# Cross-attention block on one core: W2 from seven block products a step later, exponentials by head, mask added in PSUM

## The chip, the cores and the metric

The kernel runs on one core of a Trainium2 chip. The metric is device microseconds of one execution. Its engines have in-order queues of their own: PE (matmuls and weight loads), DVE, ACT, POOL (elementwise work; POOL does not touch PSUM here), and SP, which issues most DMAs. PSUM is used as eight banks of 128 partitions by 512 float32 values, called b0 to b7 below. All data are float32.

## The reference, cut to what matters

128 sequences of 128 tokens and 256 channels, 16 heads of 16 channels, hidden width 1024:

```python
q, k, v = heads(x @ Wq + bq), heads(ctx @ Wk + bk), heads(ctx @ Wv + bv)
scores = where(j < i, q @ k.T / 4, -1e30)      # strictly below the diagonal
attn = softmax(scores); attn[row 0] = 0
x1 = layer_norm(x + (attn @ v) @ Wo + bo, ln1_g, ln1_b)
out = layer_norm(x1 + relu(x1 @ W1 + b1) @ W2 + b2, ln2_g, ln2_b)
```

## The kernel before, in words

Two sequences make a pair `p`, so there are 64 pairs. The order of every engine's instructions is the order of the calls in the text, written by hand; each engine takes its own in that order and waits for what it needs. The kernel is a pipeline over pairs: `step(p)` (L995), for p from 5 to 63, does the scores and softmax of pair p, the attention output of p-2, the hidden layer and the product with W2 of p-3, the second normalization of p-4 and the store of p-5. `third`, `fourth` and `fifth` fill the pipeline, and the lines from L1056 on empty it.

PE's order in a step is: `weigh(p-2)` (attention times values, L471 and L481, into bank 7), `scores_both(p)` (L364), `queries(p+1)` (bank 4), `attention_out(p-2)` (bank 5), `keys(p+1)` (bank 0), `values(p)` (bank 1), `hidden(p-3)` (L687, banks 2, 3, 4, 0), `second(p-3)` (L705, bank 6). The scores are split: the "high" half are the later 64 queries against all 128 keys (banks 0 to 3, four heads in each), the "low" half the first 64 queries against 64 keys (banks 6, 7, 4, 5). Rows of both sequences share the 128 partitions.

The softmax goes through all engines. `mask` (L378, DVE) adds 0 or -1e30 and copies the scores from PSUM to the tile `sm`; `maximum` is a row maximum on DVE (L389) and then a subtraction on POOL (L390); `exponential` (L397, ACT) takes 1024 elements a row at once, so three instructions serve 16 heads of both halves; `sums` adds the rows and inverts the sums on DVE (L409, L410) and multiplies on POOL (L411). `turn` (L424, DVE) transposes blocks of 32, and `bring` (L439, SP) moves them between partitions by 16 DMAs into `pT`, which `weigh` reads two steps later.

ACT also empties banks: queries (L268), keys (L279, four, each with a tile as bias and one as scale), values (L299, L304), the hidden layer's relu (L693); and it applies the normalizations `norm1` (L542) and `norm2` (L579). `turn_x1` (L651, DVE) transposes what `norm1` made, and SP's DMAs take it over DRAM to `x1T`, which `hidden` reads a step later. `second` multiplies the hidden tile `hT` (one buffer; 8 chunks of 128 channels by 256 tokens) with W2: for each of the two sequences 8 matmuls of 256 columns, summed in bank 6. `second_sum` (L715, DVE) adds the residual `x1b`, `stats` makes the mean and variance, `scale_and_shift` (POOL) the factors, `finish` (POOL) the gain and offset of the second normalization, `store` the output's DMA. In steps 28 and 51 `pad` puts empty instructions between the matmuls of `second`.

Of the kernel before, what the change touches and what calls it, by code (L numbers as in the profile page):

```python
# [8 lines left out]
F32 = mybir.dt.float32  # L9
# [4 lines left out]
P = 128  # L14
# [5 lines left out]
def tile_cross_attention_block(  # L20
# [192 lines left out]
    def bank(name):  # L213
        turns[0] += 1
        return at_bank(4 + turns[0] % 4, name)
# [179 lines left out]
    def exponential(p, hi, part):  # L395
        sm = states[p]["sm", hi]
        nc.scalar.activation(sm[:, part, :], sm[:, part, :], AF.Exp)  # L397
# [20 lines left out]
    def turn(p, hi, t):  # L418

        st = states[p]  # L420
        if "tb" not in st:
            st["tb"] = wide(f"tb_{p}").rearrange("p (j n) -> p j n", j=NS)
        at = (t if hi else 2) * 256
        nc.vector.transpose(  # L424
            st["tb"][:, :, at : at + 256].rearrange("p j (n a) -> p n j a", a=32),
            st["sm", hi].rearrange("p h j -> p (h j)")[:, t * 1024 : (t + 1) * 1024].rearrange(
                "p (n j a) -> p n j a", j=NS, a=32
            ),
        )
# [139 lines left out]
    def scale_and_shift(p):  # L569

        st = states[p]
        deviation(p, 2)
        shift(p, 2)
# [126 lines left out]
    def second(p, s, fs=range(FC), pad=0):  # L700
        st = states[p]
        if s == 0 and fs[0] == 0:
            st["py"] = at_bank(6, f"py_{p}")
        for f in fs:
            nc.tensor.matmul(  # L705
                st["py"][:, s * D : (s + 1) * D], st["hT"][:, f, s * P : (s + 1) * P],
                w2[:, f, :], start=(f == 0), stop=(f == FC - 1),
            )
            for _ in range(pad):
                nc.tensor.nop(hint="pad", nofuse=True)  # L710

    def second_sum(p):
        st = states[p]
        t2 = st["t2"] = ffn.tile([P, 2, D], F32, tag="t2", name=f"t2_{p}")
        nc.vector.tensor_tensor(  # L715
            t2, st.pop("py").rearrange("p (s d) -> p s d", s=2), st.pop("x1b"), ALU.add
        )
# [3 lines left out]

    warm = bank("warm")
    for i in range(12):
        nc.tensor.transpose(warm[:, i % 4 * P : (i % 4 + 1) * P], ident, ident)
# [237 lines left out]
    def fifth():  # L964
        p = 4
        load_ahead(p)
        scores_both(p)
        mask(p, 0, B)
        mask(p, 1, A)
        maximum(p, 1, ONE)  # L970
        queries(p + 1)
        mask(p, 1, B)
        maximum(p, 1, TWO)
        exponential(p, 1, ONE)
        mask(p, 0, A)
# [12 lines left out]
        second(1, 1)  # L988
        turn(p, 1, 0)
        turn(p, 1, 1)  # L990
        turn(p, 0, 0)
        bring(p, nc.sync, LATE_FIRST)
        hidden(2, range(FC // 2))

    def step(p):  # L995
# [35 lines left out]
        def between(f):  # L1031
            if f == (FC // 2 if p == 5 else 2):
                norm1(p - 2)
# [19 lines left out]
    for p in range(5, NP):  # L1053
        step(p)

    p = NP - 1  # L1056
    weigh(p - 1)
    context(p - 1)
    second_sum(p - 3)
    residual1(p - 2)  # L1060
    finish(p - 4)
    add_bo(p)
    hidden(p - 2, range(2))
    attention_out(p - 1)
    attention_sum(p - 1)
    attention_stats(p - 1)
    shift(p - 1, 1)
    stats(p - 3, states[p - 3]["t2"], 2)
    scale_and_shift(p - 3)
    store(p - 4)  # L1070
    hidden(p - 2, range(2, FC), lambda f: norm1(p - 1) if f == 4 else None)
    turn_x1(p - 1)
    norm2(p - 3)
    second(p - 2, 0)
    second(p - 2, 1)

    weigh(p)
    context(p)
    second_sum(p - 2)
    residual1(p - 1)  # L1080
    finish(p - 3)
    hidden(p - 1, range(2))
    attention_out(p)
    attention_sum(p)
    attention_stats(p)
    shift(p, 1)
    stats(p - 2, states[p - 2]["t2"], 2)
    scale_and_shift(p - 2)
    store(p - 3)
    hidden(p - 1, range(2, FC), lambda f: norm1(p) if f == 4 else None)  # L1090
    turn_x1(p)
    norm2(p - 2)
    residual1(p)
    finish(p - 2)
    second(p - 1, 0)
    second(p - 1, 1)
    store(p - 2)

    second_sum(p - 1)
    hidden(p, range(FC))  # L1100
    stats(p - 1, states[p - 1]["t2"], 2)
    deviation(p - 1, 2)
# [58 lines left out]
```

## Time and profile before

| | |
|---|---|
| runs | 1570.42, 1572.33, 1574.22 us; median 1572.33 |
| span of the profiled execution | 1570.3 us |
| granted TensorE clock, mean | 0.999 |
| PE busy | 1554.3 us |
| DVE busy | 1273.2 us |
| ACT busy | 802.7 us |
| POOL busy | 1304.3 us |

A row of the profile names line, engine, operation and tile, then output and input shapes, then how many, busy time, the mean length of one in ns, and the idle time of the engine ahead of them. In a timeline a row is a start, a length, and neighbouring instructions of one kind merged, with the idle time ahead of it in brackets. A matmul as written in the code stands as two MATMUL and two LDWEIGHTS (PEld, weight load) instructions. Lengths overlap on an engine: the next instruction starts before the last has written its result, so the step from start to start is what an instruction costs in a full queue, and its length is what one that needs its result waits for.

### The profile page before, as it was taken

How to read it: one execution, taken by the hardware profiler on the slowest of the kernel's cores; microseconds unless marked ns; L12 is line 12 of the kernel's file. 1: busy time of each engine (PE TensorE's matmuls, PEld its weight loads, DVE VectorE, ACT ScalarE, POOL GpSimd, SP SyncE). 2: the span in 40 equal slices, each digit the busy share in tenths (PEclk: the TensorE clock that was granted, in tenths of full speed). 3: DMA queues.
4: the chain of work that ended last, by engine and by line, in shares of the span. 5: the costliest groups of instructions: out<-in, count | busy, mean ns of one | idle time of the engine just before them, and what ended most of it. 6: DMA issues, size and time to landing. Idle time of an engine off the chain costs nothing.

```text
span 1570.3 us, 41807 instructions
## 1 busy us (share of the span) xinstructions
PE 1554.3 (99%) x16486; PEld 1347.3 (86%) x16486; DVE 1273.2 (81%) x2125; ACT 802.7 (51%) x1680; POOL 1304.3 (83%) x1229
## 2 busy tenths in 40 slices
PE   8999999999999999999999999999999999999998
PEld 7788888888888888888888888888888888888887
DVE  7988887887888888878878888888788788888853
ACT  5654544645545545446455455454454454554532
POOL 6879888888888888888888888888888888888882
PEclk9999999999999999999999999999999999999999
DMA  8356555655656555556556555555564665554441
GB/s 194 86 117 142 138 141 127 142 120 133 142 128 136 128 130 137 141 123 141 125 131 142 133 132 132 129 133 139 130 142 114 136 142 133 131 126 121 106 121 48
DMA packets 415251, 203.86 MB, mean 130 GB/s; under 512 B 282448, under 2 KB 383056, under 8 KB 415056
## 3 DMA queue, kind: packets, MB, share of 16 engines
q1 hardware_dynamic: 413152, 200.13, 55.1%
q8 instruction: 131, 2.15, 0.6%
q10 hardware_dynamic: 1904, 1.06, 0.3%
q14 instruction: 64, 0.52, 0.1%
HBM read 70.26 MB, written 33.29 MB: 66 GB/s over the span
## 4 chain that ended last, share of the span: by engine, by line
PE 89%; DVE 3%; SPq 3%; DMA 2%; issue 1%; POOL 1%; ACT 0%; ACTq 0%; POOLq 0%; DVEq 0%
PE ph L687 26%; PE py L705 25%; PE pq L257 7%; PE po L500 6%; PE pk L257 6%; PE pv L289 6%; PE pss L364 5%; PE pc L481 3%; PE pc L471 2%; SPq L439 2%; DVE tb L424 1%; DVE sm L378 1%; DMA x<-in_x_dram 1%; SPq L92 1%; DVE nmx L389 1%
## 5 line engine op out<-in xcount | busy, mean ns | idle before, releaser
L390 POOL TENSOR_TENSOR sm<-sm,nmx 128x1024 f32<-128x1024 f32 x192 | 364.2, 1897 | 130.9 <-DVE nmx L389 130.7
L687 PE MATMUL ph<-x1T,w 128*128 128x256 f32 x2048 | 453.9, 379 | 0.1
L705 PE MATMUL py<-w,hT 128*128 128x256 f32 x2016 | 447.5, 380 | 2.9 <-ACT hT L693 2.8
L687 PEld LDWEIGHTS ph<-x1T,w 128*128 128x128 f32 x2048 | 388.6, 190 | 54.0 <-ACT x1T L669 0.5
L705 PEld LDWEIGHTS py<-w,hT 128*128 128x128 f32 x2016 | 381.7, 190 | 58.7 <-ACT hT L693 4.8
L411 POOL TENSOR_TENSOR sm<-sm,rs 128x1024 f32<-128x1024 f32 x192 | 361.7, 1898 | 24.8 <-DVE rs L410 24.7
L378 DVE TENSOR_TENSOR sm<-pss,neg 128x512 f32<-128x512 f32 (+1 forms) x512 | 254.3, 549 | 89.1 <-PE pss L364 86.5
L397 ACT ACTIVATE sm<-sm 128x1024 f32<-128x1024 f32 x192 | 203.5, 1060 | 200.6 <-POOL sm L390 192.7
L389 DVE TENSOR_REDUCE nmx<-sm 128x8 f32<-128x1024 f32 (+1 forms) x192 | 232.3, 1210 | 4.6
L409 DVE TENSOR_REDUCE su<-sm 128x8 f32<-128x1024 f32 (+1 forms) x192 | 226.3, 1179 | 3.8 <-ACT sm L397 3.8
L424 DVE STREAM_TRANSPOSE tb<-sm 128x1024 f32<-128x1024 f32 x186 | 214.5, 1203 | 0.2
L493 ACT COPY cxT<-pc 128x508 f32<-128x508 f32 x64 | 37.2, 582 | 344.9 <-PE pc L481 344.9
L693 ACT ACTIVATE hT<-ph,b1e_c 128x256 f32<-128x256 f32 x504 | 197.7, 479 | 24.7 <-PE ph L687 24.7
L651 DVE STREAM_TRANSPOSE tbx<-x 128x512 f32<-128x512 f32 x63 | 44.8, 712 | 139.1 <-ACT x L542 95.9
L268 ACT ACTIVATE qT<-pq,bqs_c 128x256 f32<-128x256 f32 x126 | 52.9, 470 | 163.9 <-PE pq L257 163.9
L257 PE MATMUL pq<-xT,wq 128*128 128x256 f32 x504 | 125.5, 392 | 0.0
L279 ACT ACTIVATE kT<-pk,bkh,half 128x256 f32<-128x256 f32 x252 | 121.5, 562 | 3.8 <-PE pk L257 3.8
L500 PE MATMUL po<-wo,cxT 128*128 128x256 f32 x512 | 121.2, 379 | 0.0
L289 PE MATMUL pv<-wv,cT 128*128 128x256 f32 x512 | 121.0, 379 | 0.0
L257 PE MATMUL pk<-cT,wk 128*128 128x256 f32 x504 | 119.2, 379 | 0.0
L500 PEld LDWEIGHTS po<-wo,cxT 128*128 128x128 f32 x512 | 97.1, 190 | 13.7 <-ACT cxT L493 0.3
L289 PEld LDWEIGHTS pv<-wv,cT 128*128 128x128 f32 x512 | 97.2, 190 | 13.2
(100 smaller groups left out, 1877.0 us busy)
## 6 DMA issues: line engine op xcount, KB each, us to landing
pT<-tb SPq DMA_DIRECT2D x984, 96.0 KB, 2.2
x1t<-tbx SPq DMA_DIRECT2D x252, 64.0 KB, 1.8
x1T<-x1t SPq DMA_DIRECT2D x63, 256.0 KB, 2.8
out_dram<-t SPq DMA_DIRECT2D x63, 256.0 KB, 2.4
xb<-in_x_dram SPq DMA_DIRECT2D x124, 128.0 KB, 3.8
cb<-in_ctx_dram SPq DMA_DIRECT2D x124, 128.0 KB, 3.9
x<-in_x_dram SPq DMA_DIRECT2D x31, 512.0 KB, 4.6
w<-in_L_xattn_W_dram SPq DMA_DIRECT2D x2, 1024.0 KB, 7.3
```

The costliest lines, as they stand in the source:

```text
L257: nc.tensor.matmul(ps[:, m * TP : (m + 1) * TP], w[:, k, m * P : (m + 1) * P], src[:, k, :], start=(k == 0), stop=(k == KC - 1),)
L289: nc.tensor.matmul(pv[:, s * D : (s + 1) * D], st["cT"][:, k, s * P : (s + 1) * P], wv[:, k, :], start=(k == 0), stop=(k == KC - 1),)
L378: nc.vector.tensor_tensor(st["sm", hi][:, 4 * r : 4 * r + 4, :], st["sps", hi][r][:, : 4 * n].rearrange("p (n j) -> p n j", j=n), no[:, No ...
L389: nc.vector.tensor_reduce(nmx[:, part], sm[:, part, :], AX.X, ALU.max, negate=True)
L390: nc.gpsimd.tensor_tensor(sm[:, part, :], sm[:, part, :], nmx[:, part, None].to_broadcast([P, part.stop - part.start, n]), ALU.add,)
L397: nc.scalar.activation(sm[:, part, :], sm[:, part, :], AF.Exp)
L409: nc.vector.tensor_reduce(su, sm[:, part, :], AX.X, ALU.add)
L411: nc.gpsimd.tensor_tensor(sm[:, part, :], sm[:, part, :], rs[:, :, None].to_broadcast([P, part.stop - part.start, n]), ALU.mult,)
L424: nc.vector.transpose(st["tb"][:, :, at : at + 256].rearrange("p j (n a) -> p n j a", a=32), st["sm", hi].rearrange("p h j -> p (h j)")[:, ...
L500: nc.tensor.matmul(po[:, s * D : (s + 1) * D], cxT[:, k, s, :], wo[:, k, :], start=(k == 0), stop=(k == KC - 1),)
L687: nc.tensor.matmul(ph[:, i * TP : (i + 1) * TP].rearrange("p (s i a) -> p s i a", s=2, a=32), w1[:, k, (f + i) * P : (f + i + 1) * P], st[ ...
L705: nc.tensor.matmul(st["py"][:, s * D : (s + 1) * D], st["hT"][:, f, s * P : (s + 1) * P], w2[:, f, :], start=(f == 0), stop=(f == FC - 1),)
```

## The change

- **W2.** The product of a pair, hidden (two sequences, even and odd chunks) with W2 (two column halves, even and odd chunks), is a 2 x 2 block product. It is made from seven block products of 4 matmuls with 128 columns in place of eight, with sums and differences of blocks: of W2 once (`combine_w2`, POOL, in `fifth`), of the hidden tile for each pair (`combine_hidden`, four POOL instructions, into `hS`). The seven lie in banks 6 and 7; `sum_of_seven` adds them to the residual with five DVE instructions in place of one.
- **A step later.** The product is that of p-4 and stands on PE ahead of `hidden(p-3)`; `sum_of_seven`, `stats` and `scale_and_shift` stand last in the step; `norm2` and `finish` move to the next.
- **Exponentials.** The subtraction on POOL goes; each head's negated maximum is the bias of its own exponential: 16 of 128 elements, read from PSUM, and 16 of 64 elements.
- **Mask.** For the high half only its last 64 keys are masked, in place in PSUM, and the maxima are taken from PSUM, by bank.
- **Order.** ACT does the high exponentials, `norm2`, the queries, the low exponentials, keys, values, `norm1`, then the relus. On DVE `turn_x1` comes after the input's transposes (`tokens`), then the three turns. The `pad` goes. Steps 5 and 6 use the eight-block product, half a pair each, and the end of the kernel is rewritten (`behind`).

```diff
+    def mask_high(p, rs):
+        st = states[p]
+        for r in rs:
+            ps = st["sps", 1][r].rearrange("p (n j) -> p n j", j=P)
+            nc.vector.tensor_tensor(
+                ps[:, :, HP:], ps[:, :, HP:], neg[:, 1, None, :].to_broadcast([P, 4, HP]), ALU.add
+            )
+        for r in rs:
+            nc.vector.tensor_reduce(
+                st["nmx", 1][:, 4 * r : 4 * r + 4],
+                st["sps", 1][r].rearrange("p (n j) -> p n j", j=P), AX.X, ALU.max, negate=True,
+            )
+    def exponential_by_head(p, hi, heads):
+        st = states[p]
+        sm, nmx = st["sm", hi], st["nmx", hi]
+        for h in heads:
+            src = st["sps", 1][h // 4][:, h % 4 * P : h % 4 * P + P] if hi else sm[:, h, :]
+            nc.scalar.activation(sm[:, h, :], src, AF.Exp, bias=nmx[:, h : h + 1], scale=1.0)
+    def combine_hidden(p, engines):
+        ...
+        one.tensor_tensor(hs[:, 0], h[:, 0, 1], h[:, 1, 1], ALU.add)
+        two.tensor_tensor(hs[:, 2], h[:, 0, 0], h[:, 0, 1], ALU.subtract)
+        one.tensor_tensor(hs[:, 1], hs[:, 0], h[:, 0, 0], ALU.subtract)
+        two.tensor_tensor(hs[:, 3], h[:, 1, 0], hs[:, 1], ALU.subtract)
+    def second_by_seven(p):
+        py = st["py"] = at_bank(6, f"py_{p}")
+        pz = st["pz"] = at_bank(7, f"pz_{p}")
+        ...
+        product(py[:, :P], raw(0, 0), weights(0, 0))
+        product(pz[:, :P], raw(1, 0), weights(1, 0))
+        product(pz[:, 2 * P : 3 * P], raw(1, 1), lambda k: wt[:, 3, k])
+        product(py[:, 3 * P :], lambda k: hs[:, 0, k], lambda k: wt[:, 0, k])
+        product(py[:, 2 * P : 3 * P], lambda k: hs[:, 2, k], lambda k: wt[:, 2, k])
+        product(py[:, P : 2 * P], lambda k: hs[:, 1, k], lambda k: wt[:, 1, k])
+        product(pz[:, P : 2 * P], lambda k: hs[:, 3, k], weights(1, 1))
+    def sum_of_seven(p):
+        ...
+        add(t, x1b, 0)
+        add(t[:, 1:], t[:, 1:], 1)
+        add(t[:, 2:], t[:, 2:], 2)
+        add(t[:, 1::2], t[:, 1::2], 3)
+        nc.vector.tensor_tensor(
+            t[:, :3], t[:, :3], pz[:, : 3 * P].rearrange("p (n d) -> p n d", d=P), ALU.add
+        )
 def step(p):
         weigh(p - 2)
         context(p - 2)
         scores_both(p)
-        second_sum(p - 4)
-        residual1(p - 3)
-        finish(p - 5)
-        store(p - 5)
+        if p > 6:
+            combine_hidden(p - 4, POOL_ALONE)
         add_bo(p - 1)
         load_ahead(p)
         mask(p, 0, B)
-        mask(p, 1, A)
-        maximum(p, 1, ONE)
+        mask_high(p, A)
+        exponential_by_head(p, 1, ONES)
+        mask_high(p, B)
+        exponential_by_head(p, 1, TWOS)
+        mask(p, 0, A)
+        low_maximum(p)
+        if p > 5:
+            norm2(p - 5)
         if not last:
             queries(p + 1)
+        exponential_by_head(p, 0, range(H))
         attention_out(p - 2)
-        mask(p, 1, B)
-        maximum(p, 1, TWO)
-        exponential(p, 1, ONE)
-        mask(p, 0, A)
         attention_sum(p - 2)
         attention_stats(p - 2)
         shift(p - 2, 1)
-        maximum(p, 0, ALL)
         if not last:
             keys(p + 1)
-        exponential(p, 1, TWO)
         values(p)
-        stats(p - 4, states[p - 4]["t2"], 2)
-        scale_and_shift(p - 4)
         values_out(p)
         sums(p, 1, ONE)
-        exponential(p, 0, ALL)
         sums(p, 1, TWO)
-        hidden(p - 3, range(FC // 2 if p == 5 else 0, FC), between)
-        turn_x1(p - 2)
-        norm2(p - 4)
         sums(p, 0, ALL)
+        residual1(p - 3)
+        if p > 6:
+            second_by_seven(p - 4)
+        norm1(p - 2)
+        hidden(p - 3, range(FC // 2 if p == 5 else 0, FC))
         if p + 2 < NP:
             tokens(p + 2, "x")
             tokens(p + 2, "c")
+        turn_x1(p - 2)
         turn(p, 1, 0)
         turn(p, 1, 1)
         turn(p, 0, 0)
         bring(p, nc.sync, LATE_FIRST)
-        pad = 7 if p in (28, 51) else 0
-        second(p - 3, 0, pad=pad)
-        second(p - 3, 1, pad=pad)
+        if p > 5:
+            finish(p - 5)
+            store(p - 5)
+        if p > 6:
+            sum_of_seven(p - 4)
+        stats(p - 4, states[p - 4]["t2"], 2)
+        scale_and_shift(p - 4)
```

In the changed file `mask_high` stands at L724, `exponential_by_head` at L748, the seven products at L780, the adds of `sum_of_seven` at L808 (four) and L816 (the last).

More of the change, by code (lines that the diff above doesn't have):

```diff
@@ L724, in tile_cross_attention_block, with second_half @@
+    def second_half(p, s):
+        st = states[p]
+        py = at_bank(6, f"py_{p}_{s}")
+        for f in range(FC):
+            nc.tensor.matmul(
+                py[:, :D], st["hT"][:, f, s * P : (s + 1) * P], w2[:, f, :],
+                start=(f == 0), stop=(f == FC - 1),
+            )
+        if s == 0:
+            st["t2"] = ffn.tile([P, 2, D], F32, tag="t2", name=f"t2_{p}")
+        nc.vector.tensor_tensor(st["t2"][:, s], py[:, :D], st["x1b"][:, s], ALU.add)
     warm = bank("warm")
@@ L988, in fifth @@
         second(1, 1)
+        combine_w2()
         turn(p, 1, 0)
@@ L999, in step @@
         scores_both(p)
-        second_sum(p - 4)
-        residual1(p - 3)
-        finish(p - 5)
-        store(p - 5)
+        if p > 6:
+            combine_hidden(p - 4, POOL_ALONE)
+        if p == 5:
+            second_sum(1)
+            finish(0)
+            store(0)
         add_bo(p - 1)
@@ L1054, in tile_cross_attention_block, with behind @@
         step(p)
-    p = NP - 1
[L1057 to L1061, printed above, removed]
-    add_bo(p)
[L1063 to L1091, printed above, removed]
+    BOTH = (nc.vector, nc.gpsimd)
+    def behind(p):
+        weigh(p)
+        context(p)
+        combine_hidden(p - 2, BOTH)
+        norm2(p - 3)
+        second_by_seven(p - 2)
+        attention_out(p)
+        attention_sum(p)
+        attention_stats(p)
+        shift(p, 1)
+        residual1(p - 1)
+        finish(p - 3)
+        store(p - 3)
+        sum_of_seven(p - 2)
+        stats(p - 2, states[p - 2]["t2"], 2)
+        scale_and_shift(p - 2)
+        hidden(p - 1, range(FC), lambda f: norm1(p) if f == 0 else None)
+        turn_x1(p)
+    p = NP - 1
+    add_bo(p)
+    behind(p - 1)
+    behind(p)
+    combine_hidden(p - 1, BOTH)
     norm2(p - 2)
+    second_by_seven(p - 1)
     residual1(p)
     finish(p - 2)
-    second(p - 1, 0)
-    second(p - 1, 1)
     store(p - 2)
-    second_sum(p - 1)
+    sum_of_seven(p - 1)
     hidden(p, range(FC))
```

44 lines of the change are left out of this document (41 added, 3 removed).

## The prediction, as it was put on record before the run

> **What bounds the kernel now.** I read the page first (busy times, then the chain that ended last), then one step of the timeline, engine by engine.
>
> ```profile
> span 1570.3 us, 41807 instructions
> ## 1 busy us (share of the span) xinstructions
> PE 1554.3 (99%) x16486; PEld 1347.3 (86%) x16486; DVE 1273.2 (81%) x2125; ACT 802.7 (51%) x1680; POOL 1304.3 (83%) x1229
> ...
> PE 89%; DVE 3%; SPq 3%; DMA 2%; issue 1%; POOL 1%; ACT 0%; ACTq 0%; POOLq 0%; DVEq 0%
> ```
>
> PE is busy for 99% of the span and is 89% of the chain. The timeline of PE for one step (start, length, both in us):
>
> ```profile
> 821.50 0.43 PE L471 MATMUL pc<-pT,vd 128*32 128x64 f32 x16
> ...
> 822.97 1.62 PE L364 MATMUL pss<-kT,qT 32*64 32x128 f32 x64
> ...
> 838.44 7.07 PE L705 MATMUL py<-w,hT 128*128 128x256 f32 x32
> 845.44 0.43 PE L471 MATMUL pc<-pT,vd 128*32 128x64 f32 x16
> ```
>
> From one L471 to the next is 23.94 us, with no idle time noted. So a step is the sum of PE's work, and the product with W2 (L705) is 7.00 us of it. The other engines have room:
>
> ```profile
> 821.50:845.44 23.94, 23.94 (x257) 20.89 (x257) 19.84 (x34) 12.38 (x26) 20.36 (x20) 1.00 0.59 135
> ```
>
> The columns are length, then busy PE, weight loads, DVE, ACT, POOL: DVE 19.84, ACT 12.38, POOL 20.36 us. Two steps are longer, for their `pad`:
>
> ```profile
> 669.91 7.59 PE L705 MATMUL py<-w,hT 128*128 128x256 f32 x32
> 677.83 0.43 PE L471 MATMUL pc<-pT,vd 128*32 128x64 f32 x16 [0.33 <-DMA x1T<-x1t]
> ```
>
> Here the stretch lasts 7.92 us, 0.92 more.
>
> **PE's new sum.** A written matmul is two instructions in the trace: L705 runs 32 of 7.00/32 = 0.219 us each, with 256 columns. The change puts 7 x 4 = 28 matmuls of 128 columns in its place, 56 instructions, each with a weight load of 128 columns. The nearest rows are the transposes at the start, of 128 columns, and the loads of L705:
>
> ```profile
> 47.54 1.91 PE L454 MATMUL ptp<-ident,sm 128*128 128x128 f32 x16
> 49.28 1.89 PE L687 MATMUL ph<-x1T,w 128*128 128x256 f32 x8
> ```
>
> ```profile
> L705 PEld LDWEIGHTS py<-w,hT 128*128 128x128 f32 x2016 | 381.7, 190 | 58.7 <-ACT hT L693 4.8 <-issue 2.1 <-DVE sm L378 0.3
> ```
>
> Sixteen transposes take 1.74 us, 0.109 each, which is half of L705's 0.219. I take 0.111: 56 x 0.111 = 6.2 us, 0.8 less than 7.00. The bounds are 0.109 and the load's whole length, 0.190 (56 x 0.190 = 10.6 us), if a load can't run under the matmul ahead of it. I stay near the lower one since back-to-back transposes have loads of their own. PE's sum becomes 23.94 - 7.00 + 6.2 = 23.14 us.
>
> The Trainium skill (TensorE: Matmul & The Clock Gate, "Back-to-back issue gap") speaks against that: pairs of load and matmul with 128 columns sustain one per about 81 ns, where the matmul alone would be 56. No row here has load and matmul of equal length, so the trace can't settle it; the rival "loads" below works it out.
>
> **What the change adds is a loop that goes through ACT and DVE.** The new `sum_of_seven` reads banks 6 and 7 at the end of a step on DVE, behind the three turns, and `weigh` of the next step writes bank 7. So PE's first matmul of a step, and all that is queued behind it, waits for DVE's last add. Before, bank 7 was free since `mask(p, 0, A)`, and only `second_sum`, on bank 6, came at the step's edge. Ahead of that add, DVE waits in `turn_x1` for `norm1` on ACT, which now stands behind 32 small exponentials, `norm2`, the queries', keys' and values' copies. I go round this loop. First DVE in the same step of before:
>
> ```profile
> 823.78 1.95 DVE L378 TENSOR_TENSOR sm<-pss,neg 128x256 f32<-128x256 f32 x4 [1.49 <-PE pss L364]
> 825.76 1.22 DVE L389 TENSOR_REDUCE nmx<-sm 128x8 f32<-128x1024 f32 x1
> ...
> 829.35 0.74 DVE L378 TENSOR_TENSOR sm<-pss,neg 128x256 f32<-128x256 f32 x2
> 830.01 0.68 DVE L526 TENSOR_TENSOR t<-po,xb 128x512 f32<-128x512 f32 x1
> 830.73 0.43 DVE L513 BATCH_NORM_STATS2 bs<-t 128x6 f32<-128x256 f32 x1
> ...
> 839.02 0.71 DVE L651 STREAM_TRANSPOSE tbx<-x 128x512 f32<-128x512 f32 x1 [2.27 <-ACT x L542]
> 839.65 1.18 DVE L409 TENSOR_REDUCE su<-sm 128x16 f32<-128x1024 f32 x1
> ...
> 842.20 3.46 DVE L424 STREAM_TRANSPOSE tb<-sm 128x1024 f32<-128x1024 f32 x3
> 845.58 0.66 DVE L715 TENSOR_TENSOR t<-py,x1b 128x512 f32<-128x512 f32 x1
> ```
>
> 1. From `weigh`'s start to DVE's first mask: 823.78 - 821.50 = 2.28 us, unchanged.
> 2. DVE until ACT may start: two low masks and two high masks, the high ones now 256 wide, 0.33 each start to start (0.66 for two at 829.35), then one reduction of 512 elements. The 1024-wide one is 1.22; 512 fewer at about 1.0 ns each (512 against 256 wide: 0.68 against 0.74 - 0.33 = 0.41) leave 0.69. With 0.05 to hand over (ACT's L542 ends at 838.99, in the rows below, and DVE's L651 starts at 839.02; POOL's L390 comes 0.08 after DVE's L389): 4 x 0.33 + 0.69 + 0.05 = 2.06.
>
> ACT in that step:
>
> ```profile
> 830.01 1.93 ACT L279 ACTIVATE kT<-pk,bkh,half 128x256 f32<-128x256 f32 x4
> 831.82 1.07 ACT L397 ACTIVATE sm<-sm 128x1024 f32<-128x1024 f32 x1
> 832.77 0.65 ACT L299 COPY vz<-pv 128x256 f32<-128x256 f32 x2
> 833.28 0.76 ACT L304 COPY vd<-pv 64x256 f32<-64x256 f32 x2
> ...
> 836.46 1.55 ACT L693 ACTIVATE hT<-ph,b1e_c 128x256 f32<-128x256 f32 x4
> 837.89 1.10 ACT L542 ACTIVATE x<-t,nb,sd 128x256 f32<-128x256 f32 x2
> 838.87 1.57 ACT L693 ACTIVATE hT<-ph,b1e_c 128x256 f32<-128x256 f32 x4
> ```
>
> 3. Start to start, 256 elements: from PSUM with a bias tile (L693) 1.43/4 = 0.357; with bias and scale tiles (L279) 1.81/4 = 0.452, so a tile operand is 0.095; from SBUF with two (L542) 0.98/2 = 0.49, so with one 0.395, with none 0.30. The 1024-wide exponential takes 0.95, so an element is 0.65/768 = 0.85 ns. A high head (128, PSUM, bias) is then 0.357 - 128 x 0.00085 = **0.25**, a low one (64, SBUF, bias) 0.395 - 192 x 0.00085 = **0.235**. Sixteen of each are 7.76 us, where three exponentials took 2.9. That the fixed part stays at small widths shows in the smallest one:
>
> ```profile
> L141 ACT ACTIVATE table<-power 128x2 f32<-128x2 f32 x1 | 0.2, 203 | 0.0
> ```
>
> 203 ns for two elements; 1.07 less 1024 x 0.00085 is 0.20 too. The bounds: below, elements alone (0.11 and 0.05); above, no overlap of neighbours, +0.12 each as 1.55 - 1.43 shows (0.37 and 0.355). The Trainium skill (ScalarE: Activation LUTs, "What ACT_TABLE_LOAD costs") has 280 ns + 0.833 ns an element with a bias tile and an overlap of about 93 ns: an estimate of 0.24 for a low head, as here, but 0.29 for a high one; by it the loop would be 0.7 us longer. For PSUM the rows give less, and I keep them.
>
> ACT's stretch: 16 x 0.25 + 0.98 (`norm2`, as L542) + 2 x 0.36 (queries) + 16 x 0.235 + 1.81 (keys) + 0.51 + 0.76 (values) + 1.10 (`norm1`) + 0.04 = 13.68. What it waits for is in time: later maxima on DVE, pk and pv on PE.
>
> 4. DVE to the end: `turn_x1` 0.63, three turns 3.38 (842.20 to 845.58), five adds in a chain. A dependent one follows after its length plus 0.04 (830.01 to 830.73 is 0.72): 512 wide 0.72, 384 (0.54) twice, 256 (0.41) twice: 0.72 + 0.58 + 0.45 + 0.45 + 0.54 = 2.74 where `second_sum` was 0.66. With 0.07 to PE: 6.82.
>
> Loop: 2.28 + 2.06 + 13.68 + 6.82 = **24.84 us**, against PE's 23.14. PE would stand 1.7 us ahead of each `weigh`, and a step be 0.90 longer than 23.94.
>
> **The rest costs nothing.** On POOL three subtractions go and four combinations of 512 elements come, by these rows:
>
> ```profile
> 824.36 1.27 POOL L250 TENSOR_TENSOR xb<-x,bov_r 128x512 f32<-128x512 f32 x1
> 827.06 1.89 POOL L390 TENSOR_TENSOR sm<-sm,nmx 128x1024 f32<-128x1024 f32 x1 [1.44 <-DVE nmx L389]
> ```
>
> -5.7 + 5.1 us. The combinations start behind `scale_and_shift`, about 3 us after `weigh` starts, and end by 8.5; PE asks for the first at about 12.5, under the queries', keys', values' and raw products. If that cover went, PE would wait up to 5.1 us. `add_bo` moves behind them, for a sum one step later. `combine_w2` (5.1 us, once) has only POOL work behind it: 0, at most 5.1. `store` and its DMA move behind the 16 DMAs of `bring` on SP's queue, and the turns end some 2 us later in the step; pT is read two steps later, x1T more than half a step later, so 0. Masking in place in PSUM is costed as the mask to SBUF; within 0.1 us of it either way, 0.2 in the loop.
>
> **The sum**, against the profiled execution: its span is 1570.3, the median of the runs 1572.33, so 2.0 outside it or between runs, kept. Fifty-five steps (8 to 62) at +0.90: +49.5. Steps 5 to 7 and 63, where one or the other part is missing: 0, within 3. At the end one product more stands behind the last step, since the loop doesn't give back what the late start saved: +6.2. The pads go: -1.8. Together +54: **1626 us**.
>
> **Rivals.** *Short exponentials are cheap* (faster, 0.12; another 0.03 about level): neighbours overlap more at small widths than at 256. From 28 ns less for each of the 32 a step is below 23.94; from 53 ns on PE's 23.14 is the bound. Then steps 5 and 6, with half a product each, give back what the end adds, and 57 products at -0.8 with the pads make -47: 1525. For it: DVE has slack as soon as ACT is early (19.84 busy now). Against it: the 203 ns row. *Loads* (0.10): a matmul of 128 columns can't hide the next load. Halfway between the two bounds, at 0.150, a product is 8.4 us and PE needs 25.3 a step, over the loop: 57 x 1.4 - 1.8 = +78: 1650; at 0.190 it is +203: 1775. From 0.141 on it passes the loop. For it: the 190 ns row; against it: L454. By the ratio of the page named above, 81 to 56, an estimate of 0.158 would give 1676. *Exponentials don't overlap* (0.04): +3.8 us in the loop, 55 x 4.7 + 4 = 1835. *My loop* (0.71).
>
> **How the numbers follow.** Each 0.1 us in the loop is 5.5 us in all. The loop's terms hold to about 0.6 together, so 1592 to 1660 for my case alone; to leave out no more than 2 in 10 the range goes to 1575 below and 1690 above. About 0.2% (3 us) can be told from no change: faster 0.12, same 0.03, slower 0.85.
>
> **What would show it.** Right: PE idle about 1.7 us ahead of L471 in each step, released by DVE's last add (L816), some 95 us in all; DVE's L651 still waiting for L542; the exponentials of L748 0.24 to 0.25 apart; L780 at 0.11. Wrong: no idle time at L471 and steps of 23.1 (exponentials under 0.2), L780 over 0.14 apart, or a PE wait for POOL's hS.

## The result, and the profile after

| | before | after |
|---|---|---|
| runs, median (lowest to highest) | 1572.16 us (1570.42 to 1574.22) | 1645.77 us (1644.09 to 1649.49) |
| span of the profiled execution | 1570.3 us | 1642.4 us |
| mean granted clock | 0.999 | 0.996 |

The ratio of the runs is 1.047, with a 95% interval of 1.0452 to 1.0488. From the page of the changed kernel, the busy times and the chain that ended last:

```profile
span 1642.4 us, 47426 instructions
...
PE 1526.3 (93%) x17926; PEld 1362.6 (83%) x17926; DVE 1347.6 (82%) x2490; ACT 1116.4 (68%) x3391; POOL 1265.9 (77%) x1290
...
ACT 44%; DVE 25%; PE 18%; issue 7%; DMA 2%; SPq 2%; POOL 2%; DVEq 0%; ACTq 0%; POOLq 0%
ACT sm L748 25%; DVE tb L424 12%; DVE t L808 6%; ACT kT L279 6%; ACT x L542 4%; ACT t L579 3%; PE ph L687 3%; PE pss L364 3%; PE pc L481 3%; ACT qT L268 2%; PE pc L471 2%; DVE pss L729 2%; ACT vd L304 2%; SPq L439 2%; ACT vz L299 2%
```

PE has less to do (1526.3 us instead of 1554.3) and is no longer the bound: 18% of the chain instead of 89%. ACT is the largest part, and the exponentials by head (L748) alone are a quarter of the span. One step on PE:

```profile
802.88 0.43 PE L471 MATMUL pc<-pT,vd 128*32 128x64 f32 x16 [1.72 <-DVE t L816]
...
806.84 0.43 PE L364 MATMUL pss<-kT,qT 32*64 32x128 f32 x4 [0.91 <-issue]
...
814.22 1.05 PE L780 MATMUL py<-w,hT 128*128 128x128 f32 x8
...
820.47 7.07 PE L687 MATMUL ph<-x1T,w 128*128 128x256 f32 x32
827.96 0.43 PE L471 MATMUL pc<-pT,vd 128*32 128x64 f32 x16 [0.42 <-DVE t L816]
```

From one L471 to the next is 25.08 us, 1.14 more than before, although the product is shorter: L780 runs from 814.22 to 820.47, 6.25 us for 56 instructions. In front of L471 PE stands for the last add of `sum_of_seven` (L816): 1.72 us. The second time it is only 0.42, since this step holds a stall of 0.91 in the scores that eats most of the same slack. The waits of the whole run (engine, tile and line, what it waited for: us in all, times, longest):

```profile
DVE tbx L651 <- ACT x L542: 83.0, 59, 2.6
PE pc L471 <- DVE t L816: 81.0, 53, 2.0
```

The wait ahead of L471 and that of DVE's L651 for ACT's L542 are two places in one loop. By stretches, after minus before: the start -0.4, steps 5 to 7 +2.2, steps 8 to 62 +60.8 (in it the pads, -1.8), the two stretches from there to the last `weigh` -0.3, and from the last `weigh` to the end +9.8 (36.94 to 46.74). In all +72.1.

The loop, on ACT and then on DVE:

```profile
807.26 4.24 ACT L748 ACTIVATE sm<-pss,nmx 128x128 f32<-128x128 f32 x16 [2.13 <-PE pss L364]
811.28 1.20 ACT L579 ACTIVATE t<-t,nb,sd 128x256 f32<-128x256 f32 x2
812.26 0.95 ACT L268 ACTIVATE qT<-pq,bqs_c 128x256 f32<-128x256 f32 x2
812.98 4.00 ACT L748 ACTIVATE sm<-sm,nmx 128x64 f32<-128x64 f32 x16
816.80 2.01 ACT L279 ACTIVATE kT<-pk,bkh,half 128x256 f32<-128x256 f32 x4
...
819.11 0.82 ACT L304 COPY vd<-pv 64x256 f32<-64x256 f32 x2
819.96 1.09 ACT L542 ACTIVATE x<-t,nb,sd 128x256 f32<-128x256 f32 x2
```

```profile
805.17 0.75 DVE L378 TENSOR_TENSOR sm<-pss,neg 128x256 f32<-128x256 f32 x2 [1.13 <-PE pss L364]
...
821.08 0.71 DVE L651 STREAM_TRANSPOSE tbx<-x 128x512 f32<-128x512 f32 x1 [1.40 <-ACT x L542]
821.72 3.46 DVE L424 STREAM_TRANSPOSE tb<-sm 128x1024 f32<-128x1024 f32 x3
825.09 0.65 DVE L808 TENSOR_TENSOR t<-x1b,py 128x512 f32<-128x512 f32 x1
825.78 1.47 DVE L808 TENSOR_TENSOR t<-t,py 128x384 f32<-128x384 f32 x3
827.35 0.55 DVE L816 TENSOR_TENSOR t<-t,pz 128x384 f32<-128x384 f32 x1
```

ACT stands nowhere between 807.26 and 821.05, and DVE nowhere between 821.08 and 827.90. Once round: 2.29 (from `weigh` at 802.88 to 805.17) + 2.09 (to ACT's first exponential at 807.26) + 13.82 (to L651 at 821.08) + 6.88 (to the next `weigh` at 827.96) = 25.08, the whole step.

### The profile page after: what moved, and what is told of

Its sections match the earlier page's. It is cut to its first block, busy times and chain, and to the rows that moved or that the text cites. A ratio compares the mean times of both kernels' runs of the same rounds, so it can differ in the third digit from the quotient of the medians.

```text
span 1642.4 us, 47426 instructions
## 1 busy us (share of the span) xinstructions
PE 1526.3 (93%) x17926; PEld 1362.6 (83%) x17926; DVE 1347.6 (82%) x2490; ACT 1116.4 (68%) x3391; POOL 1265.9 (77%) x1290
## 3 DMA queue, kind: packets, MB, share of 16 engines
q10 hardware_dynamic: 1904, 1.06, 0.3%
## 4 chain that ended last, share of the span: by engine, by line
ACT 44%; DVE 25%; PE 18%; issue 7%; DMA 2%; SPq 2%; POOL 2%; DVEq 0%; ACTq 0%; POOLq 0%
ACT sm L748 25%; DVE tb L424 12%; DVE t L808 6%; ACT kT L279 6%; ACT x L542 4%; ACT t L579 3%; PE ph L687 3%; PE pss L364 3%; PE pc L481 3%; ACT qT L268 2%; PE pc L471 2%; DVE pss L729 2%; ACT vd L304 2%; SPq L439 2%; ACT vz L299 2%
## 5 line engine op out<-in xcount | busy, mean ns | idle before, releaser
L748 ACT ACTIVATE sm<-pss,nmx 128x128 f32<-128x128 f32 x944 | 250.5, 415 | 130.5 <-DVE nmx L733 87.7
L520 POOL TENSOR_SCALAR ve<-mv 128x2 f32<-128x2 f32 x127 | 29.5, 233 | 307.3 <-DVE mv L514 297.0
L748 ACT ACTIVATE sm<-sm,nmx 128x64 f32<-128x64 f32 x944 | 236.0, 443 | 0.0
L780 PE MATMUL py<-wt,hS 128*128 128x128 f32 x1440 | 172.2, 276 | 3.1 <-POOL hS L767 3.1
L780 PEld LDWEIGHTS py<-wt,hS 128*128 128x128 f32 x1440 | 166.5, 193 | 3.7 <-POOL hS L767 3.7
L378 DVE TENSOR_TENSOR sm<-pss,neg 128x256 f32<-128x256 f32 (+1 forms) x276 | 108.0, 433 | 67.8 <-PE pss L364 65.3
L733 DVE TENSOR_REDUCE nmx<-pss 128x4 f32<-128x512 f32 x236 | 150.6, 678 | 0.0
L471 PE MATMUL pc<-pT,vd 128*32 128x64 f32 x2048 | 53.8, 222 | 83.0 <-DVE t L816 81.0
L471 PEld LDWEIGHTS pc<-pT,vd 128*32 128x32 f32 x2048 | 36.5, 109 | 107.9 <-DVE t L816 103.7
L364 PE MATMUL pss<-kT,qT 32*64 32x256 f32 (+1 forms) x3840 | 103.8, 330 | 10.9 <-issue 10.3
```

Source lines behind the costliest of these rows:

```text
L364: nc.tensor.matmul(st["sps", hi][r][s * HP : (s + 1) * HP, m * 2 * n : (m + 1) * 2 * n].rearrange("p (e j) -> p e j", e=2), st["qT"][strip ...
L471: nc.tensor.matmul(pc[32 * j : 32 * j + 32, at : at + HP], st["vd"][:, s, 4 * m + j].rearrange("p e d -> p (e d)"), pT[:, 2 * s : 2 * s + ...
L733: nc.vector.tensor_reduce(st["nmx", 1][:, 4 * r : 4 * r + 4], st["sps", 1][r].rearrange("p (n j) -> p n j", j=P), AX.X, ALU.max, negate=True,)
L748: nc.scalar.activation(sm[:, h, :], src, AF.Exp, bias=nmx[:, h : h + 1], scale=1.0)
L780: nc.tensor.matmul(out, left(k), right(k), start=(k == 0), stop=(k == FC // 2 - 1))
```

## The experiments

Theory: the step is the loop `weigh`, masks, ACT, `norm1`, `turn_x1`, the turns, the adds of `sum_of_seven`, `weigh`; only the place of `sum_of_seven` and of `norm1` in it makes the change slow. Rivals: the small matmuls or the small exponentials are too dear in themselves, wherever they stand. A loop can be opened at either of its ends. The first four kernels share runs of the kernel before (median 1572.39 us), the others too in their own groups (1572.40, 1572.50 and 1572.12). Expected spans are those of the profiled execution, some 2 us below the measured times. The kernels of the old and the new softmax alone and the one with empty instructions ran once each.

### The add that reads bank 7 comes second, not last

```diff
         add(t, x1b, 0)
+        <the add of pz>
         add(t[:, 1:], t[:, 1:], 1)
         add(t[:, 2:], t[:, 2:], 2)
         add(t[:, 1::2], t[:, 1::2], 3)
-        <the add of pz>
```

> One line moved in the changed kernel: the add that reads bank 7 (pz) becomes the second of the five adds instead of the last. Theory (a loop: weigh waits for DVE's last add on bank 7, and that add waits, through turn_x1, for ACT): bank 7 is free after two adds (0.68 + 0.55 us) instead of after 2.81, before PE has finished the hidden layer, so PE no longer waits ahead of weigh. The loop then closes on DVE itself, from its first mask to the end of the second statistics, 23.9 us by the trace of the changed kernel (805.17 to 829.1): a step of 23.9 instead of 25.07, a span of about 1642 - 56 x 1.2 = 1576 us. Rival 1 (the exponentials' total work on ACT costs the time, wherever the wait shows): no change, 25.1 a step, 1642. Rival 2 (seven products cost PE more than eight): no change, 25.1.

Measured: 1599.23 us (1593.05 to 1601.10), ratio 1.0161 (1.0132 to 1.0190). Most steps are 24.11, 0.96 shorter than with the change, with some of 23.56 and every fourth or fifth near 25. PE waits for the add of pz now (moved to L813), and the rest of the adds run beside `weigh`, here on PE and DVE in one step:

```profile
228.64 0.43 PE L471 MATMUL pc<-pT,vd 128*32 128x64 f32 x16 [0.47 <-DVE t L813]
```

```profile
228.62 1.47 DVE L808 TENSOR_TENSOR t<-t,py 128x384 f32<-128x384 f32 x3
...
231.49 0.76 DVE L378 TENSOR_TENSOR sm<-pss,neg 128x256 f32<-128x256 f32 x2 [0.19 <-PE pss L364]
```

Three adds have left the path ahead of `weigh`, 1.5 us. But DVE comes to the first mask later by them: 231.49 - 228.64 = 2.85 after `weigh` instead of 2.29. That gives 0.56 back, and 25.07 - 1.5 + 0.56 = 24.1 is the step. The loop is still there, only shorter. Expected were 23.9 a step, a loop that closes on DVE alone and no wait ahead of `weigh`. But DVE's L651 waits for ACT's L542 as long as before (83.4 us in all, 83.0 with the change), so the loop still goes through ACT, and PE still waits 18.0 us in all for the add of pz.

### norm1 ahead of the keys

```diff
         shift(p - 2, 1)
+        norm1(p - 2)
         if not last:
             keys(p + 1)
 ...
-        norm1(p - 2)
         hidden(p - 3, ...)
```

> In the changed kernel norm1 stands on ACT ahead of the keys' and values' copies instead of behind them, 3.1 us earlier; nothing else moves. Theory (loop through ACT): turn_x1 on DVE waits 1.40 us for norm1 and no longer does, the loop gets 1.4 shorter, a step is 23.7, the span about 1642 - 56 x 1.4 = 1564 us. Rival 1 (ACT's total work): the work is the same, so 25.1 and 1642. Rival 2 (DVE is full): turn_x1's wait is not on the path, 25.1.

Measured: 1573.27 us (1572.07 to 1578.67), ratio 1.0012 (0.9999 to 1.0024): level with the kernel before. Plain steps are 23.53, every fourth or fifth 24.3 to 25.3. Its waits:

```profile
PE pss L364 <- issue: 10.9, 12, 1.4
...
PE pc L471 <- DVE t L816: 7.8, 42, 0.5
```

What PE waits for the last add fell from 81.0 us to 7.8. What is left in the long steps is the stall with the releaser "issue" (the profile shows nothing that PE waited for) that the step of the changed kernel showed too, 10.3 us in all. There it came out of PE's slack; here, where there is little slack, it sets back the step.

### Both

> The two edits together (bank 7's add second, norm1 ahead of keys). Theory: both ways round the loop are shorter than PE's own work, so PE has no waits and a step is PE's sum, 23.94 - 7.00 + 56 x 0.112 = 23.2 us; span about 1642 - 56 x 1.9 = 1536 us, 2% below the kernel before. Rival 1 and 2: 1642. If DVE's queue were full, about 23.9 a step and 1576.

Measured: 1557.25 us (1556.40 to 1564.58), ratio 0.9912 (0.9882 to 0.9941): faster than both kernels. The page:

```profile
PE 1525.2 (98%) x17926; PEld 1365.3 (88%) x17926; DVE 1341.1 (86%) x2490; ACT 1109.1 (71%) x3391; POOL 1265.3 (81%) x1290
...
PE 92%; DVE 3%; POOL 2%; issue 1%; DMA 1%; ACT 1%; SPq 0%; ACTq 0%; POOLq 0%; DVEq 0%
```

The same instructions take nearly the same busy time as in the changed kernel (1525.2 against 1526.3 on PE, less than 1% apart on DVE and ACT); what went is waiting. The chain is PE's again. One plain step, and ahead of it a long one:

```profile
342.31 0.43 PE L471 MATMUL pc<-pT,vd 128*32 128x64 f32 x16
...
343.79 1.57 PE L364 MATMUL pss<-kT,qT 32*64 32x128 f32 x61
346.14 0.43 PE L364 MATMUL pss<-kT,qT 32*64 32x128 f32 x3 [0.78 <-issue]
...
366.76 0.43 PE L471 MATMUL pc<-pT,vd 128*32 128x64 f32 x16
...
390.05 0.43 PE L471 MATMUL pc<-pT,vd 128*32 128x64 f32 x16
```

The plain step is 390.05 - 366.76 = 23.29 us without idle time, the long one 24.45 with 0.78 us in the scores. By stretches against the kernel before: steps 8 to 62 -27.8, steps 5 to 7 +4.1, the end +9.8 as in the changed kernel. The 1536 expected took 1.9 us off each step, where 25.07 - 23.29 is 1.78 (some 9 us in all), and had no long steps (10 us).

### The low exponentials in one instruction

```diff
-        exponential_by_head(p, 0, range(H))
+        sm = states[p]["sm", 0]
+        nc.scalar.activation(sm, sm, AF.Exp, bias=states[p]["nmx", 0][:, 0:1], scale=1.0)
```

The low half then uses the maximum of head 0 for all heads; the other 15 are left out of the exponentials.

> The changed kernel with the sixteen low exponentials in one instruction of 1024 elements, with the maximum of head 0 as the bias of all (the other fifteen low maxima are left out). ACT's work gets 16 x 0.239 - 1.0 = 2.8 us shorter. Theory: turn_x1's wait of 1.40 and the low sums' wait of 0.99 ahead of it go, the loop shrinks by 2.4 to 22.7, below PE's sum of 23.2, which then sets the step: span about 1536 us. Rival 2 (the seven products): 25.1 a step, 1642, since PE's work is unchanged. Rival 3 (the adds on DVE set the step alone, not ACT): no change, 25.1.

Measured: 1553.35 us (1550.99 to 1555.90), ratio 0.9882 (0.9856 to 0.9907). Plain steps are 23.29, the same as with the edits of the order: with about 2.8 us less on ACT, the loop passes below PE's sum without any edit of the order. Together with the edit of `norm1`, which leaves ACT's work as it is, this shows that ACT's stretch in front of `norm1` decides, and that in these kernels PE's 23.29 is what remains below it. The time missed the expected one by the long steps (some 10 us) and, as above, by 1.78 in place of 1.9; the start, steps 5 to 7 and the end gave some 5 us back.

### Eight blocks again, all else as changed

`second_by_seven` becomes the old `second`, `sum_of_seven` the old `second_sum`, and the combinations go.

> The changed kernel with the product with W2 from eight blocks as before (bank 6 alone, one add on DVE, no combinations on POOL), still a step later; exponentials by head and mask in PSUM stay. Theory (loop through bank 7): weigh has nothing to wait for, since bank 7 is free after the low mask; the way round DVE and ACT is 2.09 + 13.82 + 0.64 + 3.37 + 0.7 + 1.2 = 21.8 us, below PE's sum of 23.94, so PE sets the step at 23.94 as before and the span is 1570 plus some 8 us at the two ends: 1578. Rival (the exponentials alone cost the time): 25 a step, 1640.

Measured: 1588.79 us (1586.46 to 1589.90), ratio 1.0098 (1.0081 to 1.0114). Plain steps are 23.94, as in the kernel before: the exponentials by head, the masks in PSUM and the new order cost a step nothing as long as the sum at its end is one add on bank 6. What is over the expectation lies elsewhere: step 6 (+3.9), the end (+8.6), and seven steps of 24.4 to 25.5 (28 to 31, 57 to 59), where the scores stall with the releaser "issue". The kernel before has a `pad` in step 28, where the first of these stretches begins, and one in step 51, and no such stall.

### The old softmax in the new order, and the new softmax in the old order

The first leaves the seven products and the new order and takes masks, maxima, POOL's subtractions and three exponentials from before. The second takes the kernel before and changes only the softmax.

> The changed kernel with the softmax of before (mask copies to SBUF, maximum, subtraction on POOL, three wide exponentials), in the changed order; seven products and the combinations on POOL stay. ACT gets about 5 us a step shorter. If ACT's work were what the step waits for whatever POOL does: 23.2 to 23.5 a step, 1540. Theory (each loop by its own sum): POOL then has 20.4 + 5.1 = 25.5 us of work a step and the subtraction stands in the way from the scores to the exponentials behind the combinations, so a step is 25.5 to 27.5, and the span 1660 to 1790: by itself neither half of the change can be had in this order.

> The kernel before with exponentials by head and the mask in PSUM alone, in the order of before from step 5 on (eight products, pads, relus behind the exponentials on ACT). POOL loses 5.7 us a step, ACT gains 4.9, to 17.3. If only sums count, PE sets the step at 23.94 and nothing changes, 1570. Theory (order counts): the relus now stand behind 16 low exponentials, hT and so the product come late, and norm1, turn_x1 and the turns with them: 24.5 to 26 a step, 1600 to 1695.

Measured: 1791.91 and 1713.93 us, plain steps of 27.57 and 26.27, one run each. Both are above the ranges expected, the first by 2 us, the second by 19. In the first, the waits:

```profile
ACT sm L397 <- POOL sm L390: 419.4, 111, 9.4
...
PE pc L471 <- DVE t L816: 161.8, 57, 4.9
```

ACT waits 419.4 us for POOL's subtraction, which the change removes: in the new order the old softmax makes a longer loop than the exponentials by head do. The mean granted clock is 0.94 here: PE stands 2.8 us on the mean, at most 4.9, ahead of `weigh`, and the clock is halved for 3.4 us or twice that in nearly each step, which costs half of that time; so up to some 1.7 us of the +3.6 below are half clock. In the second kernel the adds of seven products aren't there. DVE does wait longer for `norm1` (95.9 us in all in the kernel before), as expected, but PE hardly waits for a late hT (3.2 us in all); it waits for banks:

```profile
DVE tbx L651 <- ACT x L542: 357.0, 62, 6.0
...
PE ph L687 <- ACT sm L748: 75.5, 57, 1.3
```

The high scores stay in banks 0 to 3 until each head's exponential has read them, and the hidden layer wants banks 2 and 3; that is 1.3 us in each step, and the keys wait 0.2 for bank 0. This was not the reason expected. Against 23.94 that is +3.6 us a step for the seven products with the old softmax, and +2.3 for the new softmax in the old order.

### What the stalls with releaser "issue" hang on

The kernel of both edits, with 128 empty instructions on PE at the end of step 12.

> The kernel 'both' with 128 empty instructions on PE once, ahead of step 12. It asks what the extra 0.5 to 1.2 us are that every fourth or fifth step of 'both' has, inside the scores, with no releaser. Theory (PE runs out of fetched instructions: each such stall ends 1.1 to 1.7 us after a 16 KB packet of the instruction queue; PE's 560 instructions of a step are 2.2 such packets): half a packet more moves the place of the packets' edges by half a packet, so the long steps after step 12 move by about two steps, and those ahead of it stay; their number and the span stay within 5 us of 1557. Rival (something in the data or DMAs with a period of its own, such as the loads by pairs): the same steps are long as in 'both'.

Measured: 1563.2 us in one run, a little over the 5 us allowed. The stretch with them, counted as step 11, is 29.88 us. In the kernel without them the steps over 23.7 were 11, 15, 20, 24, 29, 33, 38, 42, 47, 51 and 60. With them, behind the nops' own and the two steps after it, the steps over 23.4 are 17 (by 0.03), 18, 22, 27, 31, 35, 40, 49, 53, 58 and 62, and one at 61 that both kernels have: seven of the old ones (20, 24, 29, 33, 42, 51, 60) come two steps sooner. The steps at 35, 53 and 62 are not two ahead of an old one, and old ones at 38 and 47 have none. So they mostly hang on where in PE's stream of instructions a step lies, not on what it computes. The stream of instructions has a row of its own among the DMA queues, in the changed kernel as in that of both edits:

```profile
q8 instruction: 142, 2.33, 0.6%
```

That is 142 packets of 16 KB, one every 11 to 12 us. By the packet records, all stalls of over 0.25 us with this releaser from step 8 on, 12 in the changed kernel and 8 in that of both edits, end 1.15 to 1.61 us after a packet had been moved. The number of packets doesn't decide: the kernel before has 131 and no such stall in the scores, the one with eight blocks 131 and stalls in seven steps. That PE runs out of fetched instructions where they are shortest (`weigh` and the scores) fits all of this; it was not isolated further.

### The end of the kernel: three steps to the cause

In the changed kernel PE's end looked like a wait for the combinations on POOL:

```profile
1618.58 2.83 PE L780 MATMUL py<-wt,hS 128*128 128x128 f32 x16 [1.89 <-POOL hS L767]
1621.21 1.92 PE L780 MATMUL pz<-w,hS 128*128 128x128 f32 x8
```

Sixteen take 2.05 elsewhere and 2.83 here, eight take 1.92 instead of 1.06: behind the wait the clock is halved. Two kernels, made from the one with both edits, take the wait away: one makes the last products from eight blocks, the other does all four combinations on DVE there (`BOTH = (nc.vector, nc.vector)`).

> The kernel `both`, whose emptying of the pipeline (from the step after the last on) makes its three products from eight blocks, with one add, and without the combinations. In `both` the last weigh starts 46.74 us before the end, in the kernel before 36.94. Theory: the 9.8 us are one product more (6.25), one product shortened (-0.75), and two waits for the combinations, 0.55 and 2.04, with the half clock after the second, 1.7. Then without combinations there is no wait and no half clock: 36.94 + 7.0 = 43.9 from the last weigh to the end, the stretch between the last two weighs 17.25 instead of 17.75, the span 1555.5 - 3.3 = 1552. Rival: the end is set by the chain through the normalizations on DVE, ACT and POOL, and PE's waits only fill what would be idle anyway: 46.7 stays, span 1555.

> The kernel `both`, with all four combinations on DVE while the pipeline empties, instead of two on DVE and two on POOL. POOL's two stand behind the factors and offsets of the normalization there. Theory: the combinations come in time, no wait and no half clock: 36.94 + 6.25 - 0.75 = 42.4 us from the last weigh to the end, the stretch between the last two weighs 16.5 to 16.6 instead of 17.75, the span 1555.5 - 5.5 = 1550. A second question, about DVE's first combination, which takes 1.46 to 1.48 us where the second takes 0.69: if it is POOL working at the same time that stretches it, all four are stretched in turn when POOL works beside them, and one of 0.69 to 0.7 can only stand beside an idle POOL or beside a POOL instruction of another kind; if it is the form (two halves of the hidden tile), the next such one, hS[2], takes 1.47 as well and the other two 0.69. At 1.47 each PE still waits about 1.6 us in all: 44 to the end.

Measured: 1555.31 us (1553.81 to 1557.28) and 1555.61 us (1554.61 to 1557.28), ratios 0.9893 (0.9879 to 0.9908) and 0.9898 (0.9882 to 0.9915). PE's waits for the combinations are gone, and the stretch between the last two `weigh` fell as expected (17.75 to 17.21 and 16.56). But the end did not: 45.52 and 46.52 us, where 43.9 and 42.4 were expected. Something else was late at almost the same moment, x1T for the last hidden layer. PE waits for it 1.83 us in the kernel with eight blocks and 2.14 in that with DVE's combinations, here on PE and on SP's queue:

```profile
1531.50 8.80 PE L687 MATMUL ph<-x1T,w 128*128 128x256 f32 x32 [2.14 <-DMA x1T<-x1t]
```

```profile
1524.76 0.39 SPq L594 DMA_DIRECT2D out_dram<-t  x1
1525.25 1.90 SPq L235 DMA_DIRECT2D x1t<-tbx  x4
```

x1's transfers stand on SP behind a store, and the store waits until POOL has finished its tile (L586, from 1523.47 for 1.27 us, to 1524.74). Two more kernels tell who is at fault: the store behind x1's transfers, or attention_out ahead of the last four products.

```diff
         finish(p - 3)
-        store(p - 3)
 ...
         turn_x1(p)
+        store(p - 3)
```

> The kernel `end_dve`, with the store that stands on SP's queue ahead of the transfer of x1 while the pipeline empties moved behind it. In `end_dve` the waits for the combinations are gone, and the end didn't come earlier by them: PE waits 2.14 us for x1T of the last pair instead, with 1.7 us of half clock behind it. Its transfers start at 1525.25, though the transpose that they carry (L651) ended at 1522.49: ahead of them on SP stands the store, which waits until POOL's L586 ends at 1524.74. Theory: the transfers start at about 1522.6, 2.6 us earlier, x1T lands ahead of PE's need; no wait, no half clock, 42.6 us from the last weigh to the end instead of 46.5, the span 1552.7 - 3.8 = 1549 with the same loop. Rival: x1T's own way of 6.2 us after the transpose, or another transfer beside it, is what is late, and the wait stays over 1 us.

> The kernel `end_dve`, with attention_out of the last two pairs behind the third of the seven products instead of behind all. Everything from there to x1T (the sum, the statistics, norm1, the transpose, and POOL's work ahead of the store) comes about 3.6 us earlier, the store too. Theory (the last x1 is late, whatever holds it on SP): PE's wait for x1T goes as in `end_store`, 42.6 us from the last weigh to the end, the span 1549. Rival: POOL's L586 keeps its time, since other work stands ahead of it, then the store keeps x1 where it is: the wait stays.

Measured: 1550.99 us (1549.94 to 1552.38), ratio 0.9869 (0.9854 to 0.9884), and 1554.28 us (1551.86 to 1555.41), ratio 0.9884 (0.9868 to 0.9901). With the store moved, x1's transfers start 16.35 us after the last `weigh` instead of 19.10; from the last `weigh` to the end are 42.3 us and PE runs through, on PE and on SP:

```profile
1530.23 7.07 PE L687 MATMUL ph<-x1T,w 128*128 128x256 f32 x32
```

```profile
1523.70 1.79 SPq L235 DMA_DIRECT2D x1t<-tbx  x4
...
1527.36 10.51 SPq L594 DMA_DIRECT2D out_dram<-t  x3
```

The other kernel ends 44.0 us after its last `weigh`: its wait for x1T is gone too, but DVE's combinations have slid beside POOL's long instructions and PE waits for them. The same instructions on DVE, first beside small instructions of POOL (one element a row), then beside its long ones, and what POOL does at both times:

```profile
1511.55 0.68 DVE L767 TENSOR_TENSOR hS<-hT 128x512 f32<-128x512 f32 x1
...
1528.03 1.75 DVE L767 TENSOR_TENSOR hS<-hT 128x512 f32<-128x512 f32 x1
1529.70 1.75 DVE L768 TENSOR_TENSOR hS<-hS,hT 128x512 f32<-128x512 f32 x1
```

```profile
1511.56 2.07 POOL L565 TENSOR_SCALAR nb<-mv,sd 128x1 f32<-128x1 f32 x2
...
1526.29 1.27 POOL L554 TENSOR_TENSOR x1b<-x,g_r 128x512 f32<-128x512 f32 x1
1527.63 1.60 POOL L557 TENSOR_TENSOR x1b<-x1b,be1b_r 128x512 f32<-128x512 f32 x1
1529.19 1.71 POOL L585 TENSOR_TENSOR t<-t,g_r 128x512 f32<-128x512 f32 x1
```

That answers the second question put to the kernel before it: not the form makes a combination long on DVE, but POOL at work on long rows beside it. Beside POOL's small instructions it is POOL that is held up: the two of L565 take 2.07 us here and 0.50 elsewhere, and end with DVE's last combination (1513.63 and 1513.57).

## Why the prediction was right, step by step

- **PE would wait for the last add, a step would grow.** Right. The wait is there in 53 steps (81.0 us; some 95 had been named, and the stalls in the scores take part of the rest). Two kernels that open the loop at different places, and one that shortens ACT's part of it, each take most of it away. The loss goes with it, wholly in two of them; the add of pz alone leaves 1.6% of the 4.7%.
- **The loop's length.** Forecast 24.84, measured 25.07. Each of the four terms took a little longer than forecast: 2.28 became 2.29, 2.06 became 2.09, 13.68 became 13.82 and 6.82 became 6.88. In ACT's term the mis-sized ones are the values' second copies (0.85 in place of 0.76) and the low heads (3.82 in place of 3.76). Times 55 that is 13 us, most of the 18 by which the sum (+54) fell short of +72.
- **The small exponentials.** A high head follows the one before after (811.28 - 807.26)/16 = 0.251 us, a low one after (816.80 - 812.98)/16 = 0.239; forecast 0.25 and 0.235. The fixed part does stay at small widths, and the rival "short exponentials are cheap" falls. Of the estimates from the figures of the Trainium skill (ScalarE: Activation LUTs, "What ACT_TABLE_LOAD costs") that for the low head, 0.24, agrees; that for the high head, 0.29, doesn't, the trace has 0.251.
- **PE's product.** 6.25 us, 0.112 for each of 56 instructions; forecast 0.111. The load of 128 columns is hidden under the matmul of 128, and the rival "loads" falls. The prediction says that no row has such pairs, but its own row L454 has them, 16 loads and 16 matmuls of 128 columns at 0.109, though with loads of 142 ns instead of 190. The ratio of 81 to 56 that the Trainium skill gives for such pairs (TensorE: Matmul & The Clock Gate, "Back-to-back issue gap") isn't seen here. PE's own sum is 23.29, seen once the loop is open; forecast 23.14. Of the 0.15 between them 0.05 is the product, and 0.09 is that the hidden layer, now last in the step, takes 7.00 to the next `weigh` where it took 6.91 to the product.
- **POOL's combinations cost nothing.** Right in the steps, in which no such wait shows. Wrong at the end of the kernel, where POOL has the factors of the normalization ahead of them: waits of 0.39 and 1.89 us behind the last `weigh`, with a halved clock after the second, and one of 0.82 just ahead of it.
- **The end.** Forecast +6.2, measured +9.8 behind the last `weigh`. One product more and one shortened would be 6.25 - 0.75 = 5.5; `end_store` has 42.3 - 36.94 = 5.4. The other 4.4 had two causes at once: POOL's combinations, and x1T behind a store on SP. That x1T alone keeps the end late was measured (`end_dve`, 46.5); that the combinations alone would is argued from their waits, no kernel moves the store and leaves them on POOL. The prediction looked at this store in the step, found it free, and didn't carry it to the end, where its wait for POOL is long.
- **Steps 5 to 7 at nothing, within 3.** Measured +2.2, inside the bound partly by luck: it is -1.3, +2.4 and +1.1. Step 5 has half a product less but a wait of 3.07 us for ACT's keys; step 6 a wait of 4.21 for DVE's low mask, with 3.4 us of half clock behind it. None of this was forecast, and no run takes it apart.
- **The stalls in the scores.** Not foreseen. They cost the changed kernel little, since PE has idle time to give; the kernels in which PE hardly waits otherwise lose 9 to 14 us by the long steps.

## What to carry to other kernels

A smaller product is worth its saving only where PE stays the bound: add up, once round, everything that the next step's first matmul waits for, over all engines, before counting on it. When that loop is longer, look for the reads that can come earlier in it (the add that frees the first bank needed, the normalization ahead of copies that are not urgent): two moved calls turned a ratio of 1.047 into 0.9912. And a wait that is taken away may stand in front of another that ends almost as late; behind the last `weigh` of this kernel the first repair gained 0.2 us, and the second 4.

## What the runs showed of the hardware that was not expected

- A stall in the densest stretch of PE's instructions, 0.3 to 1.4 us of idle time (1.7 once, in `pz_first`), in every fourth or fifth step of the kernels with seven products. It moves with the place in the instruction stream (`both_nops`), and hides while PE waits for something else anyway.
- A wait of PE of 1.89 us at the changed kernel's end, and of 2.14 in `end_dve`, was followed by 3.4 us at half the granted clock; waits of up to 1.99 in the changed kernel's steps, of 1.89 at the end of `low_one` and of 3.07 in step 5 of the changed kernel were not. So a wait of about this length may cost more than itself, but its length alone doesn't decide. In each run the clock's records change only on one grid of 3.413 us. Over all 14 runs, 80 stretches of the grid at full clock held 2.0 us or more of PE idle, and all were followed by half clock; under 1.70 none of some 6300 was, and between the two 7 were and others not. The 3.07 us fall on two stretches, at most 1.72 in one. The Trainium skill (TensorE: Matmul & The Clock Gate, "HAM oscillation — how this bites in real kernels") has gaps of over about 3.4 us as those to avoid; here shorter ones were enough.
- A sum or difference of 512 elements a row from SBUF to SBUF took 0.68 us on DVE beside POOL's small instructions and 1.75 beside POOL's own of the same size, and POOL's took 1.60 to 1.71 instead of 1.27 then. DVE's adds that read PSUM showed nothing of the kind: three of L808 took 1.46 us in `end_dve` beside POOL's L554, and 1.47 in a step of the changed kernel beside an idle POOL. The Trainium skill (SBUF — State Buffer, "SBUF: two separate sides") states this: DVE with two inputs in SBUF and POOL lock a shared pair of ports against each other, for a whole instruction. The trace agrees: 1.75 is 0.68 and most of one of POOL's 1.27.
